# Graph attention and hypergraph layers on one core: the last pair's transposes, pair 61's output scaling and the last weights' sum change places

## Chip, cores and metric

The kernel runs on one core of a Trainium2 chip. The metric is the device time of one execution in microseconds, lower is better. The number compared is the median of several runs. Durations of single instructions come from one further execution, taken by the hardware profiler.

## What is computed

The input is 128 graphs of 128 nodes with 512 features each, and their 128 x 128 adjacency matrices of zeros and ones. Two layers follow each other, each with a residual sum and a layer norm.

```python
# layer 0: attention of 8 heads over the neighbours
feats = einsum('bnf,hfu->bhnu', x, W)
dense = leaky_relu(e_self[..., :, None] + e_neigh[..., None, :], 0.2) + NEG_BIG * (1 - A)
att = softmax(dense, axis=-1)
x = layernorm(x + relu(einsum('bhij,bhju->bhiu', att, feats) + b))
# layer 1: two hypergraph convolutions with a layer norm between them
def hypergraph_conv(x, adj, W, b):
    H = (adj != 0); xw = x @ W.T
    m = Be[:, :, None] * einsum('nce,nch->neh', H, xw)   # 1 / column sums of H
    return Dn[:, :, None] * einsum('nce,neh->nch', H, m) + b
h = layer_norm(relu(hypergraph_conv(x, adj, W1, b1)))    # hidden width 1024
x = layernorm(x + hypergraph_conv(h, adj, W2, b2) + x)
```

Everything is float32.

## The kernel before

Two graphs make a pair, and 64 pairs (0 to 63) run through a software pipeline. A pair's work is cut into some hundred small steps, each a Python function. Every step has a *lag* (0 to 4, in periods) and a nominal *time* within a period of T = 38.6. The list of all steps of all pairs is sorted by (pair + lag) x T + time and given out in this order (lines 1190 to 1235). These numbers are no durations: they only fix the order of instructions on each engine. Every engine takes its own instructions in that order; semaphores set by the tile framework make it wait for data and for free buffers. The tables `time = {...}` for p == LAST and p == LAST - 1 (lines 1214 to 1227) give some steps of pairs 63 and 62 other places, since at the end of the pipeline no later pair fills the gaps.

The steps that matter here, along a pair's way:

- *Attention, lags 1 and 2.* `masked` (GpSimd), `leaky` and `exponential` (ScalarE, L605 and L619) and `largest` (VectorE, L611) make the exponentials of the scores in `nb`. They go to DRAM (`e_write`, L623) and come back in blocks (`e_read`, L631, four transfers into `eb` for each of the two graphs), both issued by SyncE. `e_transpose` (VectorE, L640) turns `eb` into `eT` with two instructions for each graph, for heads 0 to 3 and 4 to 7. TensorE multiplies `eT` with the features: for the last pair in four groups (`attend`, L677), graph 0 and then graph 1, each into a PSUM bank `pav`. `attended` (L715, L716) divides by the sums, `residual` (L753) adds x, `moments` (L761, L762) takes mean and variance, `rstds` makes 1/sqrt through VectorE (L767) and GpSimd (L769, `rsa` for this norm, `rso` for the output's). `first_output` (ScalarE, L796) applies the norm.
- *First convolution, lag 3.* `propagate` (TensorE, `pz`), copies by ScalarE (L831), differences by GpSimd (`z_sums`, L842), and the product with the hidden weights. This product, like that with the output weights, is done by a scheme of seven half-size products in place of eight (`chain`, L326). Each accumulates into one of the banks X, Y and W, which are read between the products. Results: `h` (L868, VectorE, and the Relu L883, ScalarE), squares `sq` (L894, ScalarE, added up by GpSimd in L906).
- *Second convolution, lags 3 and 4.* `h_sums` (GpSimd, L469) makes four combinations `hS` of `h`. TensorE runs products 1, 2, 6, 5, 7, 4, 3 into `pyX`, `pyY` and `pyW` (L97). Product 6 reads hS number 1, product 5 number 0, product 7 number 2 and product 3 number 3. `y_sum` (VectorE, L937) joins them: its second call reads bank W after product 5, and product 3 then adds into the same bank. `y_scale` (VectorE, L1008, graph 1 and then graph 0) applies the hidden layer's norm, `output` multiplies with the propagator (TensorE, `pq`), `skip` (L807) has prepared `o`, `o_sum` (L1025) adds, `o_stats` takes the moments.
- *Output norm.* `o_norm` (VectorE, L772, two instructions, one for each graph) scales `o` in place, and `store` (SyncE, L1043) writes it. `o` has two buffers, so pair 63's `skip` writes the one that pair 61's store reads.

The last pair takes eight products in place of seven in its second convolution (`last_weigh`, L1053). For this it needs the weight block b12, of which the weights' tile holds only a difference: `last_weights` (L1046) adds two blocks on GpSimd (L1050, 128 x 1024 values). Its tile comes from the pool under the tag "hS", the buffer of `h_sums`, and its place is after pair 62's last use of it.

In the order before, GpSimd does b12 after pair 63's last z_sums; VectorE does pair 61's o_norm between pair 63's transposes of graph 0 and of graph 1:

```python
((0, 0), ..., 16.6), ((0, 1), ..., 16.65), ((1, 0), ..., 21.5), ((1, 1), ..., 21.55)  # e_transpose, lag 2
@step(4, 17.0, until=LAST)
def o_norm(p, s):
```

Of the kernel before, what the change touches and what calls it, by code (L numbers as in the profile page):

```python
# [8 lines left out]
F32 = mybir.dt.float32  # L9
# [11 lines left out]
def kernel(  # L21
# [47 lines left out]
    P = 128  # L69
# [4 lines left out]
    KH = DH // P  # L74
    HALF = 512
    QU = HALF // 2
# [7 lines left out]
    work = ctx.enter_context(tc.tile_pool(name="work", bufs=1))  # L84
# [228 lines left out]
    LAST = PAIRS - 1  # L313
# [9 lines left out]
    def at(lag, time, fn, *args, since=0, until=PAIRS):  # L323
        steps.append((lag, time, fn.__name__, range(since, until), fn, args))
# [597 lines left out]
    def weigh(s, i, to, start):  # L922
# [3 lines left out]
          QU, 1, until=LAST)  # L926
# [119 lines left out]

    def last_weights(p, s):

        b12 = work.tile([P, KH // 2, QU], F32, tag="hS", name="b12")
        nc.gpsimd.tensor_tensor(  # L1050
            b12, w2_sb[:, 4, :, :QU], w2_sb[:, 0, :, :QU], op=ALU.add
        )
        s["w2"] = ((w2_sb[:, 0], b12), (w2_sb[:, 1], w2_sb[:, 2]))  # L1053
# [68 lines left out]
            queue.dma_start(out[2 * p + g, :, cols], t)  # L1122

    for t, fn, *args in (
        (8.0, last_weights),
        (24.2, last_weigh, 0, 0), (27.8, last_weigh, 0, 1), (31.3, last_sum_squares, 0),
        (31.4, last_h_rstd, 0), (31.5, last_weigh, 1, 0), (32.5, last_scale, 0, 0),
        (32.6, last_scale, 0, 1), (34.9, last_sum_squares, 1), (35.0, last_h_rstd, 1),
        (35.1, last_output, 0, 0), (35.2, last_output, 0, 1), (35.3, last_weigh, 1, 1, (0,)),
        (35.5, last_o_sum, 0, 0), (35.6, last_scale, 1, 0), (36.0, last_o_sum, 0, 1),  # L1130
        (36.5, last_o_rstd, 0), (37.0, last_output, 1, 0), (37.1, last_weigh, 1, 1, (1,)),
        (37.2, last_o_sum, 1, 0), (38.7, last_scale, 1, 1), (38.75, last_norm, 0),
        (38.9, last_output, 1, 1), (39.6, last_o_sum, 1, 1), (40.0, last_o_rstd, 1),
        (40.5, last_norm, 1),
    ):
        at(3, t, fn, *args, since=LAST)
# [67 lines left out]
    for p in range(PAIRS):  # L1204
        if p > 1:
            todo.append(({2: 79.5, 3: 143.1, 4: 154.4}.get(p, p * T - 21.5), load, (p,)))
            todo.append(({2: 16.2, 3: 134.8, 4: 156.4}.get(p, p * T - 3.5), load_blocks, (p,)))
            todo.append(({2: 105.7, 3: 136.3, 4: 174.9}.get(p, p * T - 2.8), load_edges, (p,)))
        for lag, time, name, pairs, fn, args in steps:
            if p not in pairs:  # L1210
                continue
            if p == 0 and lag == 2 and time < 8.5:
                time *= 0.2
            if p == LAST:

                time = {
                    ("attend", 0): 24.25, ("attended", 0): 25.5,
                    ("attend", 1): 25.95, ("attended", 1): 26.0,
                    ("residual", 1): 26.3, ("rstds", "a"): 26.4,
                }.get((name,) + args[:1], time)  # L1220
            if p == LAST - 1:
                time = {
                    ("product", 2): 24.22 if (lag, time) > (3, 20.0) else time,
                    ("product", 5): 29.5 if (lag, time) > (3, 20.0) else time,
                    ("squares", 0): 26.5, ("squares", 1): 26.6, ("h_sums", 2): 22.3,
                    ("h_rstd",): 4.6, ("y_scale", 1): 5.8, ("y_scale", 0): 5.9,
                }.get((name,) + args[:1], time)
            time += (p + lag) * T
            todo.append((
                first.get((name, p) + args, first.get((name, p), time)), run, (fn, p, args)  # L1230
            ))
# [46 lines left out]
```

## Time and profile before

| what | value |
|---|---|
| median of 3 runs | 2395.36 us (2391.7, 2395.36, 2395.69) |
| profiled execution, its own time | 2392.25 us |
| its span, first to last instruction | 2390.5 us |
| granted TensorE clock, mean | 0.998 |
| busy: TensorE, its weight loads, VectorE, ScalarE, GpSimd | 99%, 81%, 87%, 64%, 76% of the span |

The span lies within the execution's own time; the 1.75 us left are before the first and after the last instruction. The page gives busy times, the chain of work that ended last, and groups of instructions by line. The timeline lists the instructions of an engine in order of time, those of one kind that follow each other merged: start, total duration, engine, line, operation, written tile <- read tiles, shape, count. In brackets stands the idle time of the engine before the group and what ended it. PE is TensorE, DVE VectorE, ACT ScalarE, POOL GpSimd, SP SyncE. A merged row hides single durations; where they matter they are given from the single instructions. Neighbouring instructions of an engine overlap by up to some 0.1 us in the records, so a start can lie a little before the end of the one before.

### The profile page before, as it was taken

The page shows a single profiled execution, that of the slowest core. Times are in us where ns is not written, and L with a number is a line of the kernel's source. Part 1 is how long each engine was busy: PE and PEld are TensorE (multiplying, and loading weights), DVE is VectorE, ACT ScalarE, POOL GpSimd, SP SyncE. Part 2 cuts the span into 40 slices and gives each one's busy share as a digit, 9 for nine tenths or more (in the row PEclk, how much of TensorE's full clock was granted, in tenths as well). Part 3 has the DMA queues.
Part 4 walks back from the last instruction along what each step waited for, and adds up shares of the span by engine and source line. Part 5 has one row for each costly group of instructions (what it writes and reads, how often), then busy time and mean ns, then how long its engine had stood idle before and what let it go on. Part 6 is the DMA issues. An engine that isn't in the chain of part 4 may idle for free.

```text
span 2390.5 us, 80668 instructions
## 1 busy us (share of the span) xinstructions
PE 2357.9 (99%) x32309; PEld 1947.1 (81%) x32309; DVE 2089.6 (87%) x4456; ACT 1529.1 (64%) x4481; POOL 1826.4 (76%) x2060
## 2 busy tenths in 40 slices
PE   7999999999999999999999999999999999999998
PEld 6777787877778878888888888888888888888886
DVE  7989888888888898898898888988988988988885
ACT  4565765756657667667667666676676676675663
POOL 5877787777777877877877778778778778777774
PEclk9999999999999999999999999999999999999999
DMA  6555554544545455555555545555555555455441
GB/s 198 138 148 148 144 149 139 155 146 143 156 144 142 148 149 149 149 146 153 142 145 153 147 144 153 150 146 142 149 149 149 148 148 145 145 153 147 140 130 37
DMA packets 431134, 347.09 MB, mean 145 GB/s; under 512 B 151440, under 2 KB 380328, under 8 KB 430760
## 3 DMA queue, kind: packets, MB, share of 16 engines
q1 hardware_dynamic: 427288, 337.46, 49.2%
q8 instruction: 256, 4.19, 0.7%
q10 hardware_dynamic: 3472, 4.47, 0.6%
q14 instruction: 118, 0.97, 0.2%
HBM read 239.08 MB, written 102.73 MB: 143 GB/s over the span
## 4 chain that ended last, share of the span: by engine, by line
PE 90%; DMA 3%; DVE 3%; ACT 1%; POOL 1%; issue 1%; SPq 0%; DVEq 0%; POOLq 0%; ACTq 0%
PE phX L97 18%; PE pyX L97 16%; PE pfX L97 9%; PE phW L97 9%; PE pyW L97 8%; PE pfW L97 5%; PE phY L97 4%; PE pq L97 4%; PE pav L705 4%; PE pz L97 4%; PE pyY L97 4%; PE pfY L97 2%; DMA nb<-rd 2%; DMA rd<-rows 1%; PE pd L97 1%; PE pf L523 1%
## 5 line engine op out<-in xcount | busy, mean ns | idle before, releaser
L344 ACT COPY py<-pyX 128x257 f32<-128x257 f32 x189 | 70.7, 374 | 531.1 <-PE pyX L97 452.2
L97 PEld LDWEIGHTS phX<-zS,w_sb 128*64 128x64 f32 x6144 | 347.9, 137 | 38.0 <-POOL ft L744 22.8
L97 PE MATMUL phX<-zS,w_sb 128*64 128x128 f32 x6144 | 371.0, 273 | 2.9 <-ACT ph L344 2.9
L906 POOL TENSOR_TENSOR sq<-sq 128x512 f32<-128x512 f32 (+2 forms) x384 | 343.9, 896 | 20.1
L589 POOL TENSOR_TENSOR nb<-nb,neg 128x512 f32<-128x512 f32 x256 | 319.9, 1283 | 31.8 <-DMA nb<-rd 29.4
L605 ACT ACTIVATE nb<-nb,ft 128x128 f32<-128x128 f32 x1020 | 325.2, 392 | 18.3 <-POOL nb L589 16.5
L619 ACT ACTIVATE nb<-nb,nm 128x128 f32<-128x128 f32 x1024 | 319.3, 391 | 5.2 <-DVE nm L611 5.1
L769 POOL TENSOR_TENSOR rso<-veo,mhalf 128x2 f32<-128x2 f32 x63 | 44.2, 702 | 337.6 <-DVE veo L767 337.6
L97 PE MATMUL pyX<-w_sb,h 128*64 128x257 f32 x2016 | 242.0, 379 | 0.5 <-ACT py L344 0.5
L97 PE MATMUL pyX<-w_sb,hS 128*64 128x257 f32 x2016 | 242.0, 379 | 0.0
L97 PE MATMUL pyW<-w_sb,hS 128*64 128x256 f32 x2016 | 241.4, 379 | 0.1
L883 ACT ACTIVATE h<-h,vecs 128x128 f32<-128x128 f32 x768 | 239.7, 393 | 2.3 <-DVE h L868 1.4
L611 DVE TENSOR_REDUCE nm<-nb 128x4 f32<-128x512 f32 x256 | 175.3, 685 | 52.3 <-ACT nb L605 39.9
L97 PEld LDWEIGHTS pyX<-w_sb,h 128*64 128x64 f32 x2016 | 159.4, 136 | 60.5 <-ACT py L344 0.9
L744 POOL TENSOR_TENSOR ft<-ft,b_bc 128x512 f32<-128x512 f32 x128 | 203.7, 1611 | 5.9 <-ACT ft L533 5.9
L97 PEld LDWEIGHTS pyW<-w_sb,hS 128*64 128x64 f32 x2016 | 159.3, 136 | 59.3 <-issue 0.9
L97 PEld LDWEIGHTS pyX<-w_sb,hS 128*64 128x64 f32 x2016 | 153.2, 136 | 51.9
L640 DVE STREAM_TRANSPOSE eT<-eb 128x512 f32<-128x512 f32 x252 | 163.5, 685 | 2.1 <-DMA eb<-ed 1.2
L1008 DVE SCALAR_TENSOR_TENSOR y<-y,rsh,bw_bc 128x512 f32<-128x512 f32 x126 | 150.1, 1229 | 17.4 <-POOL rsh L1004 17.4
L807 DVE SCALAR_TENSOR_TENSOR o<-y,b_bc 128x512 f32<-128x512 f32 x128 | 165.0, 1327 | 0.0
L469 POOL TENSOR_TENSOR hS<-h 128x512 f32<-128x512 f32 x126 | 162.3, 1288 | 0.0
L894 ACT ACTIVATE sq<-h 128x512 f32<-128x512 f32 x256 | 160.7, 629 | 2.1
(178 smaller groups left out, 5610.1 us busy)
## 6 DMA issues: line engine op xcount, KB each, us to landing
nb<-rd SPq DMA_DIRECT2D x127, 512.0 KB, 5.9
ed<-nb SPq DMA_DIRECT2D x126, 512.0 KB, 2.8
eb<-ed SPq DMA_DIRECT2D x504, 128.0 KB, 2.9
x<-in_x_dram SPq DMA_DIRECT2D x64, 512.0 KB, 4.3
out_dram<-o SPq DMA_DIRECT2D x63, 512.0 KB, 3.8
xb<-in_x_dram SPq DMA_DIRECT2D x248, 128.0 KB, 2.9
a<-in_adj_dram SPq DMA_DIRECT2D x64, 128.0 KB
w<-in_adj_dram SPq DMA_DIRECT2D x128, 64.0 KB, 4.0
```

The costliest lines, as they stand in the source:

```text
L97: nc.tensor.matmul(to[rows], lhs[:, rows], rhs, start=start, stop=stop, skip_group_check=True)
L469: engine.tensor_tensor(t[:, i], in0, in1, op=op)
L589: nc.gpsimd.tensor_tensor(t, t, neg[:, :, None, :].to_broadcast([P, NB, HH, B]), op=ALU.add)
L605: nc.scalar.activation(t, t, AF.Prelu, bias=s["ft"][:, g, h, 0:1], alpha=SLOPE)
L611: nc.vector.tensor_reduce(s["nm"][:, g, hs], scores(p, s, g, hs).rearrange("p b h j -> p h b j"), AX.XY, ALU.max, negate=True,)
L619: nc.scalar.activation(t, t, AF.Exp, bias=s["nm"][:, g, h:h + 1])
L640: nc.vector.transpose(s["eT"][:, g, hs, :].rearrange("p h (b i) -> p h b i", b=NB), s["eb", g][:, :, hs, :].rearrange("p b h j -> p h b j"),)
L744: nc.gpsimd.tensor_tensor(t, t, b0_bc.rearrange("p (h u) -> p h u", h=H), op=ALU.add)
L807: nc.vector.scalar_tensor_tensor(s["o"][:, g, :], s["y"][:, g, :], 2.0, b2_bc, op0=ALU.mult, op1=ALU.add)
L883: nc.scalar.activation(dst[:, k, :], src[:, k, :], AF.Relu, bias=b1_sb[:, c:c + 1])
L894: nc.scalar.activation(s["sq"][:, g, q * KH // 2:(q + 1) * KH // 2, :], hid(s, g, q), AF.Square, scale=DH ** -0.5,)
L906: nc.gpsimd.tensor_tensor(t[:, :n, :], t[:, :n, :], t[:, n:2 * n, :], op=ALU.add)
```

## The change

Two steps move, and one tile changes its buffer. `last_weights` goes from time 8.0 to -29.5 at lag 3, which puts it almost a period earlier; its tile b12 takes the buffer of tag "xS" (combinations of the transposed input for the feature product, of the same size, last used by pair 63's features) in place of "hS". Pair 63's transposes for graph 1 go from 21.5 and 21.55 to 16.9. Pair 61's o_norm and store go to 26.7 and 26.8, behind pair 63's moments and the VectorE part of its rstds.

```diff
     def last_weights(p, s):
 
-        b12 = work.tile([P, KH // 2, QU], F32, tag="hS", name="b12")
+        b12 = work.tile([P, KH // 2, QU], F32, tag="xS", name="b12")
         nc.gpsimd.tensor_tensor(
             b12, w2_sb[:, 4, :, :QU], w2_sb[:, 0, :, :QU], op=ALU.add
         )
...
     for t, fn, *args in (
-        (8.0, last_weights),
+        (-29.5, last_weights),
...
             if p == LAST:
 
                 time = {
                     ("attend", 0): 24.25, ("attended", 0): 25.5,
                     ("attend", 1): 25.95, ("attended", 1): 26.0,
-                    ("residual", 1): 26.3, ("rstds", "a"): 26.4,
+                    ("residual", 1): 26.3, ("rstds", "a"): 26.4, ("e_transpose", 1): 16.9,
                 }.get((name,) + args[:1], time)
+            if p == LAST - 2:
+                time = {("o_norm",): 26.7, ("store",): 26.8}.get((name,) + args[:1], time)
             if p == LAST - 1:
```

In the resulting order of each engine, VectorE runs pair 63's four transposes one after the other, then attended, residual and moments, then the two instructions of pair 61's o_norm, then pair 62's y sums. GpSimd runs b12 after pair 63's add_bias (L744) and before pair 61's rso. The order on TensorE, ScalarE and SyncE is the same as before.

## Prediction

> **What bounds the kernel now.** I began with the page. TensorE is busy almost throughout, and nine tenths of the chain that ended last is its own work:
>
> ```profile
> span 2390.5 us, 80668 instructions
> PE 2357.9 (99%) x32309; PEld 1947.1 (81%) x32309; DVE 2089.6 (87%) x4456; ACT 1529.1 (64%) x4481; POOL 1826.4 (76%) x2060
> PE 90%; DMA 3%; DVE 3%; ACT 1%; POOL 1%; issue 1%; SPq 0%; DVEq 0%; POOLq 0%; ACTq 0%
> ```
>
> So a change outside TensorE pays only where TensorE stands still. The timeline of TensorE over the last 106 us (start, duration, then the idle time before in brackets) has four such places over 0.1 us:
>
> ```profile
> 2336.23 1.33 PE L677 MATMUL pav<-ft,eT 128*64 128x65 f32 x32
> 2339.83 1.28 PE L677 MATMUL pav<-ft,eT 128*64 128x65 f32 x32 [2.27 <-DVE eT L640]
> 2340.91 1.94 PE L97 MATMUL pyX<-w_sb,hS 128*64 128x257 f32 x16
> ...
> 2346.77 1.95 PE L97 MATMUL pyX<-w_sb,h 128*64 128x256 f32 x16 [0.46 <-ACT py L344]
> 2348.56 1.90 PE L97 MATMUL pyW<-w_sb,hS 128*64 128x256 f32 x16
> ...
> 2362.10 1.94 PE L97 MATMUL pq<-y,R 128*64 128x512 f32 x8 [0.61 <-DVE y L1008]
> ...
> 2384.10 0.65 PE L97 MATMUL pq<-y_last,R 128*64 128x256 f32 x4 [0.59 <-DVE y_last L1090]
> ```
>
> The 2.27 us is pair 63's attention waiting for its second graph's transposed exponentials; the 0.61 us is pair 62's output product waiting for y_scale. VectorE over the same time shows what stands before each:
>
> ```profile
> 2335.37 1.31 DVE L640 STREAM_TRANSPOSE eT<-eb 128x512 f32<-128x512 f32 x2
> 2336.60 2.46 DVE L772 TENSOR_SCALAR o<-o,mvo,rso 128x512 f32<-128x512 f32 x2
> 2338.99 1.29 DVE L640 STREAM_TRANSPOSE eT<-eb 128x512 f32<-128x512 f32 x2
> ...
> 2345.54 0.17 DVE L767 TENSOR_SCALAR vea<-mva 128x2 f32<-128x2 f32 x1
> 2345.62 0.42 DVE L937 TENSOR_TENSOR y<-py,pyY 128x257 f32<-128x257 f32 x1
> 2346.75 0.42 DVE L937 TENSOR_TENSOR y<-py,pyW 128x256 f32<-128x256 f32 x1 [0.72 <-ACT py L344]
> ...
> 2357.98 3.97 DVE L1008 SCALAR_TENSOR_TENSOR y<-y,rsh,bw_bc 128x512 f32<-128x512 f32 x2 [1.42 <-POOL rsh L1004]
> ```
>
> Pair 61's scaling (L772) lies between the two groups of transposes. And GpSimd:
>
> ```profile
> 2323.25 2.78 POOL L744 TENSOR_TENSOR ft<-ft,b_bc 128x512 f32<-128x512 f32 x2
> 2335.44 0.70 POOL L769 TENSOR_TENSOR rso<-veo,mhalf 128x2 f32<-128x2 f32 x1 [9.41 <-DVE veo L767]
> 2336.11 1.27 POOL L469 TENSOR_TENSOR hS<-h 128x512 f32<-128x512 f32 x1
> 2337.46 1.32 POOL L469 TENSOR_TENSOR hS<-hS,h 128x512 f32<-128x512 f32 x1
> 2338.74 1.45 POOL L469 TENSOR_TENSOR hS<-h 128x512 f32<-128x512 f32 x1
> 2340.16 1.26 POOL L469 TENSOR_TENSOR hS<-h,hS 128x512 f32<-128x512 f32 x1
> ...
> 2358.60 2.81 POOL L1050 TENSOR_TENSOR b<-w_sb 128x1024 f32<-128x1024 f32 x1
> ```
>
> The reader should see the 9.41 us hole at 2326.03, and b12 (L1050) exactly under the slow y_scale at the end.
>
> **What the Trainium skill says.** "SBUF — State Buffer", section "Who interferes with whom": a Vector instruction with two SBUF inputs, or a tensor_scalar in a two-port mode, and a GpSimd instruction reading SBUF shut each other out; whoever starts first has the shared ports for the whole instruction. The trace agrees. Taken singly, the two y_scale instructions of the L1008 row last 1.207 and 2.843 us (the row's minimum is 0.884); the second ends 0.55 us after b12. Pair 62's residual (L753) took 1.817 us beside GpSimd, pair 63's 0.679 beside an idle one. The section also says that an instruction with one SBUF input does not contend: L640 keeps to 0.658 to 0.712 us in all 252 instances, L611 to 0.672 to 0.689 in 256. "PSUM — Partial Sum Buffer", section "Engine vs sequencer instructions": Vector and GpSimd queues are strictly first in, first out, and matmuls start in program order. So a moved step delays all behind it. The 2.27 us is such a case.
>
> **The change, part by part.** The order of instructions differs at two places only, one on VectorE and one on GpSimd; TensorE, ScalarE and SyncE keep theirs.
>
> *Transposes first.* The second group starts at 2336.60 instead of 2338.99, 2.39 us earlier, if its data is there. The chain of waits has the last eb transfer landing at 2336.25, and VectorE's sequencer passed its wait at 2336.33: there, with 0.3 us to spare. The first of the group ends at 2337.30, and the matmuls start 0.145 us later (2339.828 after 2339.683 in the trace), at 2337.44, where TensorE comes free anyway (its last pav matmul started at 2337.34). The matmuls end their issue 2.39 us earlier, and the next product could start at 2338.52 instead of 2340.91.
>
> *What is late next.* That product is number 6 and reads hS sum 1. In the single rows this sum began at 2337.458; without L772 beside it I give it the uncontended 1.27 us: 2338.73, and 0.09 to TensorE: 2338.82. Net 2.1 us gained, not 2.39. Products 5 and 7 need sums 0 and 2 (done by 2339.97), long there. ScalarE's copy between 7 and 4 stays (0.46 us). Product 3 (the pyW at 2348.56) could thus start at 2346.47.
>
> *The scaling's new place.* Product 3 reuses the bank that the second y sum (L937 at 2346.75) must first read, and the two L772 now stand ahead of both sums. VectorE: after the transposes all comes 2.39 us earlier, so the residual L753 starts at 2339.98 and vea ends at 2343.32. But GpSimd's last hS starts at about 2339.92, just before L753, so L753 probably waits for it, as pair 62's did: 1.1 us more (1.817 less 0.679), 2344.4. Bounds: 0 if VectorE gets in first, 2.2 if both residuals are hit. Then L772 twice: 1.94 us in the pair before, 2.46 here, extremes of the row 0.712 and 1.480 each; I take 2.2, to 2346.5. The sums take 0.34 and 0.42, to 2347.3, and 0.1 to TensorE: 2347.4, against 2346.47. A new stall of 0.9 us (bounds 0 and 1.7). Behind L772 wait only these sums; rsa (GpSimd) and ScalarE's first_output, which make y for pz, depend on vea and are done by about 2347.7, before pz at 2349.1.
>
> *The store.* Its SyncE issue moves from 2339.09 to about 2346.6. Only later stores queue behind it, and the buffer's next writer, skip of pair 63 (2362.47), has over 10 us. Cost 0. If that cover went, skip would wait for the landing, 3.8 us.
>
> *b12.* It leaves 2358.60 and fills the hole at 2326.03. There, under its 2.8 us, L807 (two SBUF inputs) waits: with L1008 ending at 2326.58 and b12 then needing 2.25, to 2328.84, L807 ends near 2330.1 instead of 2328.4, and the h sum L868 after it about 1.1 us late. ScalarE's Relus lose 0.75 us, but TensorE asks for h(0,1) only at 2334.36, against 2332.84 plus 0.75. L611, which the exponentials and so the transfer wait for, comes before L807. Cost 0; if the cover were thinner, up to 1.1 us. At the old place the second y_scale falls from 2.84 to at most 1.2 us and ends at least 1.6 us earlier; TensorE waited 0.61. Gain 0.6; nothing else was late there (skip and the next h sum follow y_scale and move forward with it).
>
> *Sum:* −2.1 + 0.9 − 0.6 = **−1.8 us**. The profiled execution took 2392.25 us (span 2390.5 and 1.75 around it) and would take 2390.4. The median of the runs is 2395.36, 3.1 above it; on that scale the forecast is 2393.6.
>
> **The rivals.**
> 1. *The sums are on time* (VectorE gets the ports at 2339.98, or L772 is fast): no new stall, −2.7 us, 2392.7. For it: a margin of 60 ns decides. Against: pair 62's 1.817.
> 2. *Mostly given back:* the stall at pyW nears 1.7, or the last eb lands later than by the 0.3 us in hand, so that the transfer becomes the gate. About −0.7 us, 2394.7.
> 3. *Slower:* the scaling queued ahead of the y sums costs TensorE more at pyW than both gains. Place: product 3. Price: both residuals blocked (2.28), L772 at 1.48 twice (2.9), sums to 2349.1: a stall of 2.8; a third block of the 2.84 us kind adds 1. It decides once the second y sum ends after 2349.0. Then +0.1 to +1.1 us, say 2396.0. Against it: GpSimd is idle during the second residual in this order.
> 4. *The scaling isn't what the transposes wait for:* excluded by the timeline, L640 following L772 with no gap.
>
> **How the numbers follow.** Forecast 0.50, rival 1 0.25, rival 2 0.18, rival 3 0.07. A change within 0.2% (4.8 us) is about what a measurement of this kernel cannot tell from none. All cases lie inside it; what takes the result out is the spread of runs: 2391.7, 2395.36, 2395.69, and 2392.25 for the profiled one. If the median after falls on the lower level (about 0.35), the forecast and rival 1 read 2389.9 and 2389.0, more than 0.2% down: 0.35 times 0.75 gives 0.25 for faster. Slower needs 2400.2: 0.03. The range: 2389.0 (rival 1 on the lower level) to 2396.3 (rival 3, or no gain on the highest run).
>
> **What would show it.** The 2.27 us gap before the second pav group gone and L640 four in a row from 2335.4; under 0.4 us before the first hS product; L772 right after vea and 0.3 to 1.5 us of idle before the last pyW, put down to y L937; L1050 near 2326 with longer L807 beside it; the 0.61 before pq gone and y_scale's pair under 2.5 us. The forecast is wrong if L640 waits for eb, if the pyW gap exceeds 2 us, or if the gap before pq stays.

## The result, and the profile after

The changed kernel takes 2390.21 us (median of 21 runs, 2386.98 to 2391.98). The kernel before takes 2393.99 us in as many runs beside it. The ratio of the two sets of runs is 0.9983, with a 95% interval of 0.9977 to 0.9989: 4.1 us faster, between 2.6 and 5.5. The two medians alone differ by 3.8 us. The profiled execution took 2389.21 us, 3.04 less than that of before.

TensorE's timeline at the end of the changed kernel, in the columns used before:

```profile
2316.32 1.94 PE L97 MATMUL pz<-R,y 128*64 128x128 f32 x32
...
2336.09 2.63 PE L677 MATMUL pav<-ft,eT 128*64 128x65 f32 x64
2338.65 1.96 PE L97 MATMUL pyX<-w_sb,hS 128*64 128x257 f32 x16
2340.44 1.90 PE L97 MATMUL pyW<-w_sb,hS 128*64 128x256 f32 x16
2342.17 1.90 PE L97 MATMUL pyX<-w_sb,hS 128*64 128x256 f32 x16
2344.55 1.95 PE L97 MATMUL pyX<-w_sb,h 128*64 128x256 f32 x16 [0.47 <-ACT py L344]
2346.33 1.90 PE L97 MATMUL pyW<-w_sb,hS 128*64 128x256 f32 x16
...
2359.09 1.89 PE L97 MATMUL pq<-y,R 128*64 128x512 f32 x8
...
2381.05 0.65 PE L97 MATMUL pq<-y_last,R 128*64 128x256 f32 x4 [0.59 <-DVE y_last L1090]
```

The two groups of pav are one row now: the 2.27 us between them are gone. So is the wait ahead of pq. No bracket stands at the last pyW, where the forecast put a new stall. The two gaps that the change doesn't touch are as before.

VectorE:

```profile
2326.95 2.87 DVE L807 SCALAR_TENSOR_TENSOR o<-y,b_bc 128x512 f32<-128x512 f32 x2
...
2335.22 2.66 DVE L640 STREAM_TRANSPOSE eT<-eb 128x512 f32<-128x512 f32 x4
...
2339.97 1.63 DVE L753 SCALAR_TENSOR_TENSOR y<-y,x 128x512 f32<-128x512 f32 x1
...
2344.11 0.17 DVE L767 TENSOR_SCALAR vea<-mva 128x2 f32<-128x2 f32 x1
2344.18 1.00 DVE L772 TENSOR_SCALAR o<-o,mvo,rso 128x512 f32<-128x512 f32 x2
2345.10 0.42 DVE L937 TENSOR_TENSOR y<-py,pyY 128x257 f32<-128x257 f32 x1
2345.43 0.41 DVE L937 TENSOR_TENSOR y<-py,pyW 128x256 f32<-128x256 f32 x1
...
2355.74 1.88 DVE L1008 SCALAR_TENSOR_TENSOR y<-y,rsh,bw_bc 128x512 f32<-128x512 f32 x2 [1.41 <-POOL rsh L1004]
```

The four transposes follow each other, with no scaling between them. The scaling (L772) takes 1.00 us where it took 2.46. y_scale takes 1.88 where it took 3.97. L807 pays 1.6 us more for b12 beside it (2.87 in place of 1.28). GpSimd shows the other side:

```profile
2325.85 2.82 POOL L1050 TENSOR_TENSOR b<-w_sb 128x1024 f32<-128x1024 f32 x1
2335.30 0.70 POOL L769 TENSOR_TENSOR rso<-veo,mhalf 128x2 f32<-128x2 f32 x1 [6.63 <-DVE veo L767]
2335.97 1.28 POOL L469 TENSOR_TENSOR hS<-h 128x512 f32<-128x512 f32 x1
2337.32 1.28 POOL L469 TENSOR_TENSOR hS<-hS,h 128x512 f32<-128x512 f32 x1
2338.55 1.27 POOL L469 TENSOR_TENSOR hS<-h 128x512 f32<-128x512 f32 x1
2339.78 1.27 POOL L469 TENSOR_TENSOR hS<-h,hS 128x512 f32<-128x512 f32 x1
2344.35 0.93 POOL L769 TENSOR_TENSOR rsa<-vea,mhalf 128x2 f32<-128x2 f32 x1 [3.30 <-DVE vea L767]
2345.25 5.21 POOL L906 TENSOR_TENSOR sq<-sq 128x512 f32<-128x512 f32 x6
```

**A measure for the end alone.** Up to pair 62's propagate (the first pz above) every engine does the same work in both kernels. Executions of one kernel reach it at times that differ by up to 1.8 us (2316.32 and 2314.51 in the two profiles of the changed kernel). So I use the *tail*: the span less the start of that pz. In the kernel before, this is the row

```profile
2316.47 1.94 PE L97 MATMUL pz<-R,y 128*64 128x128 f32 x32
```

Before: 2390.464 − 2316.467 = 74.00 us. After: 2387.423 − 2316.320 = 71.10 us. The tail says −2.90.

### The profile page after: what moved, and what is told of

It reads as the page before. It is cut to its first block, busy times and chain, and to the rows that moved or that the text cites. A ratio compares the mean times of both kernels' runs of the same rounds, so it can differ in the third digit from the quotient of the medians.

```text
span 2387.4 us, 80667 instructions
## 1 busy us (share of the span) xinstructions
PE 2357.5 (99%) x32309; PEld 1941.2 (81%) x32309; DVE 2089.5 (88%) x4456; ACT 1528.3 (64%) x4481; POOL 1824.8 (76%) x2060
## 4 chain that ended last, share of the span: by engine, by line
PE 91%; DMA 3%; DVE 3%; ACT 1%; issue 1%; SPq 1%; POOL 0%; DVEq 0%; POOLq 0%; ACTq 0%
PE phX L97 18%; PE pyX L97 17%; PE phW L97 9%; PE pfX L97 9%; PE pyW L97 8%; PE phY L97 4%; PE pfW L97 4%; PE pq L97 4%; PE pav L705 4%; PE pz L97 4%; PE pyY L97 4%; PE pfY L97 2%; DMA nb<-rd 1%; PE pd L97 1%; DMA rd<-rows 1%; PE pf L523 1%
## 5 line engine op out<-in xcount | busy, mean ns | idle before, releaser
L589 POOL TENSOR_TENSOR nb<-nb,neg 128x512 f32<-128x512 f32 x256 | 319.8, 1281 | 29.5 <-DMA nb<-rd 26.5
L744 POOL TENSOR_TENSOR ft<-ft,b_bc 128x512 f32<-128x512 f32 x128 | 203.9, 1612 | 6.0 <-ACT ft L533 6.0
L807 DVE SCALAR_TENSOR_TENSOR o<-y,b_bc 128x512 f32<-128x512 f32 x128 | 166.7, 1341 | 0.0
```

The source lines that it names most:

```text
L589: nc.gpsimd.tensor_tensor(t, t, neg[:, :, None, :].to_broadcast([P, NB, HH, B]), op=ALU.add)
L744: nc.gpsimd.tensor_tensor(t, t, b0_bc.rearrange("p (h u) -> p h u", h=H), op=ALU.add)
L807: nc.vector.scalar_tensor_tensor(s["o"][:, g, :], s["y"][:, g, :], 2.0, b2_bc, op0=ALU.mult, op1=ALU.add)
```

## Experiments

Two series were run, each on one chip with the kernel before beside it: the changed kernel again, order alone, b12 alone and scaling between (before: 2390.45 us), and then the rest (before: 2391.3 us). Absolute times are compared only within a series.

| kernel | median, us | ratio to before (95% interval) | tail, us |
|---|---|---|---|
| before | | | 74.00 |
| before, measured against itself | 2390.77 | 1.0000 (0.9992 to 1.0008) | 73.98 |
| changed, again | 2386.90 | 0.9985 (0.9979 to 0.9992) | 71.08 |
| order alone | 2387.74 | 0.9985 (0.9978 to 0.9991) | 71.89 |
| b12 alone | 2389.29 | 0.9995 (0.9987 to 1.0003) | 73.16 |
| scaling between | 2387.58 | 0.9986 (0.9978 to 0.9993) | 71.37 |
| scaling behind the sums | 2387.82 | 0.9985 (0.9978 to 0.9991) | 71.09 |
| scaling doubled | 2388.52 | 0.9990 (0.9983 to 0.9996) | 72.64 |
| copy gap filled | 2387.03 | 0.9983 (0.9976 to 0.9989) | 70.45 |

### Order alone

The changed kernel with b12 back in its old place and buffer:

```diff
-        b12 = work.tile([P, KH // 2, QU], F32, tag="xS", name="b12")
+        b12 = work.tile([P, KH // 2, QU], F32, tag="hS", name="b12")
...
-        (-29.5, last_weights),
+        (8.0, last_weights),
```

> Transposes ahead and the scaling with its store behind the moments; b12 stays where it was. If the tail's two gaps are the whole effect: the 2.27 us before the second pav group is gone, the hS product starts 2.1 us earlier, the gap before pq stays at 0.6 to 0.8, so -2.1 us against before. If something outside the tail gives part of the measured -4: up to -3.

The tail is 2.11 us shorter. TensorE and VectorE show what stays:

```profile
2333.86 2.46 PE L677 MATMUL pav<-ft,eT 128*64 128x65 f32 x64
2336.42 1.96 PE L97 MATMUL pyX<-w_sb,hS 128*64 128x257 f32 x16
...
2357.64 1.94 PE L97 MATMUL pq<-y,R 128*64 128x512 f32 x8 [0.61 <-DVE y L1008]
```

```profile
2353.52 3.98 DVE L1008 SCALAR_TENSOR_TENSOR y<-y,rsh,bw_bc 128x512 f32<-128x512 f32 x2 [1.41 <-POOL rsh L1004]
```

pav is in one piece, and the wait for y_scale is untouched. The new order accounts for the first of the two gaps and for nothing of the second.

### b12 alone

The kernel before with b12 in its new place and buffer:

```diff
-        b12 = work.tile([P, KH // 2, QU], F32, tag="hS", name="b12")
+        b12 = work.tile([P, KH // 2, QU], F32, tag="xS", name="b12")
...
-        (8.0, last_weights),
+        (-29.5, last_weights),
```

> b12 early and in the other buffer, all else as before. If the tail's gaps are the whole effect: y_scale's pair takes 1.9 us in place of 4.0, the gap before pq is gone, -0.8 us against before; the 2.27 us before pav stays. If b12's old place cost more than that gap, or its new place costs something (the longer skip of pair 62): -1.5 or 0.

The tail is 0.84 us shorter. By the whole time alone (0.9987 to 1.0003) this part can't be told from no change. The profile can tell, first on TensorE and then on VectorE:

```profile
2338.15 1.28 PE L677 MATMUL pav<-ft,eT 128*64 128x65 f32 x32 [2.32 <-DVE eT L640]
...
2359.64 1.89 PE L97 MATMUL pq<-y,R 128*64 128x512 f32 x8
```

```profile
2356.29 1.88 DVE L1008 SCALAR_TENSOR_TENSOR y<-y,rsh,bw_bc 128x512 f32<-128x512 f32 x2 [1.41 <-POOL rsh L1004]
```

The bracket at pav is there, that at pq is gone. The parts sum to 2.11 + 0.84 = 2.95 us against 2.90 for the whole: within 0.05 us they simply add up.

### Scaling between

The changed kernel with pair 61's scaling and store where they were, which is now behind the transposes:

```diff
-            if p == LAST - 2:
-                time = {("o_norm",): 26.7, ("store",): 26.8}.get((name,) + args[:1], time)
```

> The transposes ahead and b12 early, but the scaling directly behind the transposes (ahead of the attention's division). If only the transposes' place counts: the same -2.9 as the whole change in a profile. If the scaling's place counts: beside the hS sums it takes about 2.4 us again, the second y sum ends about 1.4 us later than in the whole change, a gap of 0.7 to 1.1 us opens before the last pyW, and the total is -1.8 to -2.2.

The tail is 71.37 us, 0.27 longer than that of the whole change, where 0.7 to 1.1 had been expected. VectorE:

```profile
2335.76 2.66 DVE L772 TENSOR_SCALAR o<-o,mvo,rso 128x512 f32<-128x512 f32 x2
...
2340.53 0.68 DVE L753 SCALAR_TENSOR_TENSOR y<-y,x 128x512 f32<-128x512 f32 x1
...
2344.12 0.41 DVE L937 TENSOR_TENSOR y<-py,pyW 128x256 f32<-128x256 f32 x1
```

The last two hS sums on GpSimd, and products 4 and 3 on TensorE:

```profile
2336.67 1.46 POOL L469 TENSOR_TENSOR hS<-h 128x512 f32<-128x512 f32 x1
2338.10 1.45 POOL L469 TENSOR_TENSOR hS<-h,hS 128x512 f32<-128x512 f32 x1
```

```profile
2342.67 1.95 PE L97 MATMUL pyX<-w_sb,h 128*64 128x256 f32 x16 [0.47 <-ACT py L344]
2344.68 1.95 PE L97 MATMUL pyW<-w_sb,hS 128*64 128x256 f32 x16
```

The scaling is slow again beside the hS sums, 1.66 us more than in the changed kernel. But it pushes L753 past those sums, and L753 then takes 0.68 us, where it took 1.63 and 1.80 in the two profiles of the changed kernel. So 0.95 to 1.12 us come back. Counted from pz, the second y sum ends 0.57 us later than in the changed kernel (30.09 against 29.52 us), not 1.4 as expected. It ends at 2344.53, 0.15 us before the last pyW. This pyW starts 2.01 us after the product ahead of it, in place of 1.78 in the changed kernel (2344.55 to 2346.33): it is held up by 0.23 us, although no bracket marks it. Of the 2.90 us, 0.27 depend on the scaling's place behind the moments.

### Scaling behind the sums

The changed kernel with pair 61's scaling and store later still:

```diff
-                time = {("o_norm",): 26.7, ("store",): 26.8}...
+                time = {("o_norm",): 34.0, ("store",): 34.1}...
```

> Pair 61's scaling and store behind pair 62's first two y sums, all else as changed. If the scaling ahead of the sums costs nothing because it has the ports to itself: tail 71.1 us as in the changed kernel, and the two scalings, now beside GpSimd's squares, take 1.9 to 2.5 us in place of 1.0. If the sums were late for TensorE: a shorter tail, by up to 0.3.

The tail is 71.09 us, that of the changed kernel: ahead of the sums the scaling costs nothing. Beside the squares it takes longer:

```profile
2343.24 0.42 DVE L937 TENSOR_TENSOR y<-py,pyW 128x256 f32<-128x256 f32 x1
2343.57 1.96 DVE L772 TENSOR_SCALAR o<-o,mvo,rso 128x512 f32<-128x512 f32 x2
```

Taken singly, the two scalings took 0.540 and 1.505 us. The first got in ahead of GpSimd's first square and the second did not.

### Scaling doubled

The changed kernel with the same scaling once more, its result unused:

```diff
         for g in range(2):
             normalize(s, "o", s["o"][:, g, :], g)
+        if p == LAST - 2:
+            t = work.tile([P, 2, F], F32, tag="xb", name="again")
+            for g in range(2):
+                nc.vector.tensor_scalar(
+                    t[:, g, :], s["o"][:, g, :], s["mv", "o"][:, g, 0:1],
+                    s["rs", "o"][:, g:g + 1], op0=ALU.subtract, op1=ALU.mult,
+                )
```

> Pair 61's scaling done a second time into a scratch tile, right behind the first, ahead of the y sums: added work. In the changed kernel the second y sum ends at 2345.84 and the last pyW starts at 2346.33, so about 0.4 us is in hand. If the forecast stall is real and only its size was off: the second y sum ends 1.0 us later (GpSimd shut out) to 2.5 us later (the scaling shut out), a gap of 0.6 to 2.1 us ahead of the last pyW, and the tail is 71.7 to 73.2. If the sums don't hold that product: no gap and 71.1.

VectorE, then TensorE:

```profile
2342.07 1.00 DVE L772 TENSOR_SCALAR o<-o,mvo,rso 128x512 f32<-128x512 f32 x2
2342.99 1.95 DVE L1043 TENSOR_SCALAR again<-o,mvo,rso 128x512 f32<-128x512 f32 x2
2344.86 0.41 DVE L937 TENSOR_TENSOR y<-py,pyY 128x257 f32<-128x257 f32 x1
2345.19 0.41 DVE L937 TENSOR_TENSOR y<-py,pyW 128x256 f32<-128x256 f32 x1
```

```profile
2345.75 1.95 PE L97 MATMUL pyW<-w_sb,hS 128*64 128x256 f32 x16 [1.36 <-DVE y L937]
```

Taken singly, the four scalings took 0.543, 0.541, 0.541 and 1.497 us: three pass in 0.54, and the fourth ends 0.29 us after GpSimd's first square, for which it seems to have waited. That adds 1.87 us ahead of the sums (2344.86 − 2342.99), and the tail grows by 1.54, both within what was expected. So time spent ahead of the sums does reach TensorE at pyW, and the changed kernel has 1.87 − 1.54 = 0.33 us in hand there. Its single times agree: the second y sum ends at 2345.84, pyW starts at 2346.33, and 0.15 us pass here between the end of the sum and pyW. The forecast's 2.2 us for the scaling is 1.2 more than the 1.00 measured; less the 0.33 in hand, that is its 0.9 us.

### The kernel before against itself, and the changed kernel again

No edit in either.

> The kernel before, unchanged, measured against itself in the same way as the other kernels. In the first three kernels and the changed one the whole time fell by 0.7 to 1.3 us more than the tail of their profiles (from pair 62's pz to the end) did. If that is an offset of the measurement, or drift between runs: this one reads about -0.5 to -1 too. If the changes do save something outside the tail: 0, within 0.4.

> The changed kernel again, beside its parts on the same chip. If the tail is all: -2.9 us, the sum of the parts. If there is more to it: -4, and the parts' sum falls short or one of them shows it.

The control's ratio is 1.0000, in an interval of 0.8 per thousand (1.9 us) either way, but its median is 0.5 us lower, which the expectation named as the sign of an offset. So the control doesn't decide between the two. The tails repeat within 0.02 us. By the medians, the whole times of the changed kernel fell by 3.8 and 3.6 us in its two series, 0.9 and 0.7 more than its tail; those of the other versions fell by 0.2 to 1.4 us more than theirs. The tail's 2.9 us (a ratio of 0.9988) lies in both intervals of the changed kernel. Whether the rest is scatter, an offset of the measurement or a saving before pair 62 isn't settled.

### Copy gap filled

The changed kernel with other places for steps of pairs 63, 61 and 62, in this order:

```diff
-                    ("attend", 1): 25.95, ("attended", 1): 26.0,
-                    ("residual", 1): 26.3, ("rstds", "a"): 26.4, ...
+                    ("attend", 1): 25.95 if args[1:] == (0,) else 28.0, ("attended", 1): 28.1,
+                    ("residual", 1): 28.2, ("rstds", "a"): 28.3, ...
...
-                time = {("o_norm",): 26.7, ("store",): 26.8}...
+                time = {("rstds", "o"): 28.35, ("o_norm",): 34.0, ("store",): 34.1}...
...
-                    ("product", 5): 29.5 if (lag, time) > (3, 20.0) else time,
-                    ("squares", 0): 26.5, ("squares", 1): 26.6, ...
+                    ("squares", 0): 28.5, ("squares", 1): 28.6, ...
```

> A version meant to take the next gap: product 5 goes back behind product 7, so that it covers ScalarE's copy (0.47 us), and the last attention group goes between products 6 and 7 to cover the copy there; pair 61's rso goes behind the hS sums and its scaling behind the y sums. If the gap is a matter of order: it is gone, the hS product starts about 0.5 us earlier, tail 70.5 to 70.6. If the attention's division or hS sum 2 is then late: the gap comes back ahead of product 7 or pz, tail 71 or more.

```profile
2338.00 1.96 PE L97 MATMUL pyX<-w_sb,hS 128*64 128x257 f32 x16
2339.80 0.64 PE L677 MATMUL pav<-ft,eT 128*64 128x65 f32 x16
2340.59 1.95 PE L97 MATMUL pyX<-w_sb,hS 128*64 128x256 f32 x16 [0.16 <-ACT py L344]
2342.34 1.93 PE L97 MATMUL pyW<-w_sb,hS 128*64 128x256 f32 x16
2344.07 1.93 PE L97 MATMUL pyX<-w_sb,h 128*64 128x256 f32 x16
```

Product 5 (pyW) now lies between products 7 and 4 and covers ScalarE's copy: product 4 starts 1.73 us after the product ahead of it (2342.34 to 2344.07), where the changed kernel needs 2.38 (2342.17 to 2344.55). This 0.65 us is the gain: the tail is 70.45 us, the shortest of all, as forecast within 0.05. The new wait of 0.16 us ahead of product 7 costs nothing on balance. TensorE is through with the four attention groups and product 6 when product 7 starts, 24.13 us after pz; the changed kernel, after the same work, starts product 5 at 24.12. In the whole time this difference (0.03%) is smaller than the intervals, so only the profile shows it.

## Why the prediction was right, and where it was not

The forecast was −1.8 us, the tail measured −2.90. The measured time lies in the range, and the change lies within the 0.2% that were held likeliest. That says little about the mechanism, since the range, 7.3 us wide, held the forecast and every rival. The forecast of 2393.6 us is 3.4 above the 2390.21 measured: 1.4 because the median before was 2393.99 in 21 runs and not 2395.36 as in three, 1.1 from the terms below, and 0.9 that the tail doesn't explain. Step by step:

- **Transposes first: right, but with less in hand than written.** Pair 62's pz lies 0.15 us earlier in this execution, so a time in it reads 0.15 later on the old scale. The second group was to start at 2336.60 and started at 2336.58, which is 2336.73 on the old scale. Its data was not there in time: VectorE's sequencer passed its last wait for `eb` only at 2336.54, so the 0.3 us in hand was gone and the transfer held the group for 0.13 us, as rival 2 had feared. In the second profile of the changed kernel and with the order alone, this wait ended 0.2 us before VectorE came free. It cost nothing, because hS sum 1 came last, as written: it ends at 2338.60 and the hS product starts at 2338.65. The product, forecast for 2338.82, came at 2338.80 on the old scale. Its part, forecast at 2.1, is 2.11 in the kernel with the order alone.
- **The residual waits for hS: right.** L753 took 1.63 us (forecast 1.78) and ended 0.55 us after the last hS sum. vea ended at 2344.42 on the old scale (forecast 2344.4).
- **The scaling's new place: the term that was mis-sized.** The prediction took 2.2 us for L772 "twice" and got a new stall of 0.9 us at pyW. It took 1.00, and the stall is 0. The 2.2 came from rows in which GpSimd was adding squares or hS sums at the same time. At the new place GpSimd is idle, because its next instruction, rsa, waits for vea, which ends as the scaling starts. So VectorE has the ports first, and it is rsa that waits (0.93 in place of 0.70). Each scaling takes 0.54 us, less than the row's minimum of 0.712 over all 126 instances before, which I had used as the lower end: each of those 126 overlaps a GpSimd sum. The doubled scaling showed that the stall does come once the time is really spent.
- **b12: right in place, a little small in size.** L807 ended at 2329.97 on the old scale (forecast 2330.1) without cost to TensorE (its next product, pyX, comes at 2332.62 in both). y_scale's second instruction took 0.742 us in place of 2.843. The gain was 0.84 us and not 0.6: the bracket of 0.61 counts from the modelled end of the last matmul, 0.17 us after the point from which the next could have started (2359.57 + 1.75 = 2361.32, against a start at 2362.10). This accounts for 0.78 of the 0.84.
- **The store: right.** Nothing waited for it.

What happened is rival 1 (−2.7) by the second of its two conditions, "L772 is fast"; the first, that VectorE gets the ports at 2339.98, failed. Rival 3, and rival 2 by its first condition, needed a stall at pyW, where 0.33 us was to spare. Rival 2's second condition, a late eb, was met in this execution and had no cost.

The trace agrees with what the Trainium skill's "SBUF — State Buffer" says in "Who interferes with whom", that the first to start has the ports for its whole instruction: 0.54 against 1.5 us for the same scaling, by what GpSimd was doing.

## What to carry to other kernels

A duration taken from a profile holds for its neighbours in that profile. Before you price a moved VectorE instruction with two inputs or a tensor_scalar, look at what GpSimd does at the new place and which of the two arrives first. Judge a saving of 0.1% at a program's end by a stretch of the profile that starts at a common landmark: here it repeated within 0.02 us, where medians of 13 to 21 runs were uncertain by 1.4 to 1.9.

## What the runs showed of the hardware

A float32 tensor_scalar over 128x512 takes 0.54 us where GpSimd doesn't hold it up and up to 1.5 us beside a GpSimd sum of 1.27 us. The exclusion works both ways: the last two hS sums took 1.46 and 1.45 us beside the slow scaling and 1.27 without it, and rsa, on 128x2 values, 0.93 in place of 0.70. I hadn't expected that slowing an instruction can cost little on a shared port: with the scaling between, it lost 1.66 us and L753 behind it gained at least 0.95, since the GpSimd work they both met had run out.
